# The first slot's rows in a routed feed-forward layer: gathered by a list of six columns instead of picked by products of one-hots

## The chip, the cores and the metric

The kernel runs on one core of one Trainium2 chip. The metric is device time in microseconds (us) for one execution. The kernel before takes 511.28 us, the median of three runs (511.26, 511.28 and 512.25).

## The reference

There are 2048 nodes with 256 values each and 67584 weighted edges. The kernel computes a graph layer and then a routed feed-forward layer on its result:

```
x = x + segment_sum(edge_weight[:, None] * layernorm(x)[dst], src) + node_vec1   # graph layer
t = layernorm(x)                                     # 2048 tokens of 256 values
logits = t @ Wr + br                                 # 8 experts
p, e = top_2(softmax(logits));  w = p / p.sum()
y_e = gelu((layernorm(t) * g_e + b_e) @ W1[e] + b1[e]) @ W2[e] + b2[e]      # 256 -> 1024 -> 256
x = x + w[0] * y_e[0] + w[1] * y_e[1]
```

(each token goes to two of eight experts, and each expert's weights are two matrices of 1 MB.)

## The kernel before

**Graph stage.** The edges are turned into dense 128-column blocks of an adjacency matrix, and the matrix product of these blocks with the normalised rows is summed into `acc`, which holds 16 blocks of 128 tokens. The blocks of the adjacency come in groups. `dense(blocks, b)` (line 368) issues the products of some groups for the two token blocks `b` and `b + 1` into a PSUM tile, and `add` (line 377) sums that tile into `acc`. The last of these products, for groups 4 and 3, run from line 1095 on and are interleaved with the routing, since token block after token block becomes final there.

**Routing.** The tokens are routed in two batches: the first has ten token blocks (`NA = 10`), the last has six. For a batch, in this order:

- `square` and `roots` (lines 692 and 703): ScalarE sums squares and takes roots.
- `scales` (711): reciprocals on VectorE; ScalarE writes the normalised rows into `rec`; SP stores the residual rows into `y_d` in memory.
- `logits`, `best` (twice), `shares` (724, 731, 773): the two best experts of each token and their odds. `shares` needs the Exp table on ScalarE.
- `count` and `sum_counts` (746, 760): which tokens chose which expert (`sel`), and, by products with a triangle of ones, how many earlier tokens chose the same expert. The result `pc` is a token's place in its expert's list.
- `set_shares` (779): the two weights go into the last columns of `rec`, and `rec` is stored in memory as `xr_d` by one DMA.
- `places` (788): the expert's list and the place in it, as two numbers per choice ("spots").
- `enlist` (803): one-hots of the two spot numbers, `in_lo` and `in_hi`, the latter times the token's number. `list_rows` (820): 20 products of these one-hots give `listed`, a table with the token number for every place in every expert's list.

**Slots.** The feed-forward layer runs over slots of 256 tokens of one expert. Three early slots (`whole[0]` to `whole[2]`, experts 0 to 2) are filled from the first batch alone, so that the layer can start before the second batch is routed. A slot needs its weights (`get_weights`, 939, on SP's queue), its rows (`get_rows`, 946: two indirect gathers of 128 rows each from `xr_d`, issued by GpSimd), `head` (974: four transposes of the rows on TensorE, `scale_rows` from PSUM into `xeT` on VectorE, `set_weights`), `layer_1` (1007: 16 products into eight PSUM tiles, each followed by a Gelu on ScalarE) and `layer_2` (1022: 16 products, `ys` on VectorE, an accumulating scatter into `y_d` by GpSimd).

**The first slot is filled in another way.** For `whole[0]` no rows are gathered for the products. `choose` (827) compares the places of expert 0 with 256 numbers and so makes one-hots `chosen`, ten blocks of 128 x 256; `choose_rows` (838) multiplies `rec` by them, 20 products, which gives the transposed rows at once:

```
for j in range(NA):
    for k in range(KD):
        nc.tensor.matmul(pt[:, k, :], s["rec"][:, j, k * P:(k + 1) * P], chosen[:, j, :], ...)
```

`early` (848) reads `listed` afterwards and gathers the rows of all three early slots, in the order 1, 0, 2. Those of slot 0 serve only its weights in `set_weights`.

**What sets the order.** From line 686 on the order on TensorE, VectorE, ScalarE and SP is the one in which the program issues the instructions (`manual_schedule`); GpSimd's queue holds here only the gathers and scatters. Every engine works its own queue in order, and waits at its head for semaphores of others. On TensorE the order around the change is: products of `dense` for token blocks 0 to 12, `sum_counts`, `dense` for blocks 14 and 15, `choose_rows`, `list_rows`, `layer_1` of slot 0, the transposes of slot 1, `layer_2` of slot 0 with the last batch's `sum_counts` in its middle.

Of the kernel before, what the change touches and what calls it, by code (L numbers as in the profile page):

```python
# [15 lines left out]
OP = mybir.AluOpType  # L16
# [11 lines left out]
def kernel(  # L28
# [339 lines left out]
    def dense(blocks, b):  # L368

        pa = ps_s.tile([P, 2, 512], F32, name="py1")  # L370
        for i in range(2):
            for c in blocks:
                nc.tensor.matmul(pa[:, i, :DX], acs[c][:, b + i, :], xn(c),  # L373
                                 start=(c == blocks[0]), stop=(c == blocks[-1]))
        return b, pa
# [310 lines left out]
    with tc.manual_schedule(engines=ALL - {ET.Pool}):  # L686
        listed = ps_r.tile([P, 2, P], F32, name="listed")
# [23 lines left out]
        def scales(s):  # L711
            b0 = s["b"]
            s["r"] = r = route.tile([P, 2, s["n"]], F32, name=f"r{s['i']}", bufs=1)
            nc.vector.reciprocal(r, s["sd"])  # L714
            ms = route.tile([P, s["n"]], F32, name=f"ms{s['i']}", bufs=1)
            nc.vector.tensor_mul(ms, less_m[:, b0:b0 + s["n"]], r[:, 1, :])
            s["rec"] = rec = route.tile([P, s["n"], RW], F32, name=f"rec{s['i']}", bufs=1)
            for j in range(s["n"]):
                nc.scalar.activation(rec[:, j, :D], acc[:, b0 + j, :D], AF.Identity,
                                     bias=ms[:, j:j + 1], scale=r[:, 1, j:j + 1])  # L720
            nc.sync.dma_start(y_d[:N, :].rearrange("(b p) d -> p b d", p=P)[:, b0:b0 + s["n"], :],
                              acc[:, b0:b0 + s["n"], :D])
# [23 lines left out]
        def count(s):  # L746

            hit = s["hit"]
            s["sel"] = sel = route.tile(s["full"], BF16, name=f"sel{s['i']}", bufs=1)
            nc.vector.tensor_add(sel, hit[:, :, 0, :], hit[:, :, 1, :])  # L750
            seen_b = route.tile([P, NE], BF16, name=f"seen_b{s['i']}", bufs=1)
            nc.vector.tensor_copy(seen_b, seen)
            s["seen"] = seen_b
            more = route.tile([P, NE], F32, name=f"more{s['i']}", bufs=1)
            nc.vector.tensor_reduce(more, sel.rearrange("p b e -> p e b"), AX.X, OP.add)
            nc.vector.tensor_add(seen, seen, more)
            s["seen_t"] = seen_t = route.tile([P, NE], BF16, name=f"seen_t{s['i']}", bufs=1)
            nc.vector.tensor_copy(seen_t, seen)

        def sum_counts(s):  # L760
# [10 lines left out]
            nc.tensor.matmul(s["all"], ones_b, s["seen_t"], start=True, stop=True)  # L771
# [7 lines left out]
        def set_shares(s):  # L779
            e, rec = s["odds"], s["rec"]  # L780
            both = route.tile([P, s["n"]], F32, name=f"both{s['i']}", bufs=1)
            nc.vector.tensor_scalar(both, e, 1.0, None, op0=OP.add)
            nc.vector.reciprocal(rec[:, :, D + 2], both)
            nc.vector.tensor_mul(rec[:, :, D + 3], e, rec[:, :, D + 2])
            nc.sync.dma_start(
                xr_d[:N, :].rearrange("(b p) c -> p b c", p=P)[:, s["b"]:s["b"] + s["n"], :], rec)
# [16 lines left out]
        def enlist(s):  # L803
# [3 lines left out]
            split = lambda t: t.rearrange("p n (a t) -> p n a t", t=2)  # L807
            each = iota_h[:, None, :].rearrange("p o (a t) -> p o a t", t=2).to_broadcast(hot)
            in_lo = route.tile([P, 2 * NA, P], F16, name="in_lo", bufs=1)[:, :n, :]
            nc.vector.tensor_tensor(split(in_lo), s["spots"][:, 0, :, None, :].to_broadcast(hot),  # L810
                                    each, OP.is_equal)
            in_hi = route.tile([P, 2 * NA, P], F16, name="in_hi", bufs=1)[:, :n, :]
            nc.vector.tensor_tensor(split(in_hi), s["spots"][:, 1, :, None, :].to_broadcast(hot),
                                    each, OP.is_equal)
# [3 lines left out]
            s["in"] = in_lo, in_hi  # L818
# [8 lines left out]
        def choose(s):  # L827

            pos = route.tile([P, NA], F32, name="pos", bufs=1)
            nc.vector.scalar_tensor_tensor(pos, s["pc"][:, :, 0], 1.0, s["sel"][:, :, 0],  # L830
                                           op0=OP.add, op1=OP.mult)
            for h in range(2):
                j = slice(h * NA // 2, (h + 1) * NA // 2)
                n = [P, NA // 2, TS]
                nc.vector.tensor_tensor(chosen[:, j, :], pos[:, j, None].to_broadcast(n),
                                        place1[:, None, :].to_broadcast(n), OP.is_equal)

        def choose_rows(s):

            pt = ps_x.tile([P, KD, TS], F32, name="px")  # L840
            for j in range(NA):
                for k in range(KD):
                    nc.tensor.matmul(pt[:, k, :], s["rec"][:, j, k * P:(k + 1) * P],  # L843
                                     chosen[:, j, :], start=(j == 0 and k == 0),
                                     stop=(j == NA - 1 and k == KD - 1))
            return pt

        def early(ps):
# [6 lines left out]
                tk, listed[:, 0, :].rearrange("p (e t) -> p e t", e=NE)[:, :EARLY, :TT],  # L855
# [5 lines left out]
            for u in (1, 0, 2):  # L861
# [3 lines left out]
            nc.scalar.copy(lists_0, listed[:, 0, :])  # L865

        def slots(ps):
# [39 lines left out]
            for i, r in spans:  # L907
# [25 lines left out]
        place1 = route.tile([P, TS], F32, name="place1", bufs=1)  # L933
        nc.gpsimd.iota(place1, pattern=[[1, TS]], base=1, channel_multiplier=0,
                       allow_small_or_imprecise_dtypes=True)
        chosen = route.tile([P, NA, TS], F32, name="chosen", bufs=1)
# [37 lines left out]
        def head(s):  # L974
# [8 lines left out]
            scale_rows(s, pt)  # L983
            set_weights(s)
# [92 lines left out]
        late.append(dense(GROUPS[4], 0))  # L1077
        for p in range(NP):
            if p + 1 < NP:
                late.append(dense(GROUPS[4] if 2 * p + 2 < NA else last, 2 * p + 2))  # L1080
# [3 lines left out]
            if p == NA // 2 - 1:  # L1084
                roots(first_b)
                scales(first_b)
                logits(first_b)
                best(first_b, 0)
            elif p == NA // 2:
                best(first_b, 1)  # L1090
                count(first_b)
                sum_counts(first_b)
                shares(first_b)
                nc.scalar.activation(warm, eps_sb, AF.Sqrt)
            elif p == NA // 2 + 1:
                choose(first_b)
# [3 lines left out]
        set_shares(first_b)  # L1100
        places(first_b)
        roots(last_b)
        enlist(first_b)
        pt = choose_rows(first_b)
        scale_rows(whole[0], pt)
        list_rows(first_b)
        hT = layer_1(whole[0])
        early(first_b["all"])
        scales(last_b)
        logits(last_b)  # L1110
# [4 lines left out]
        count(last_b)  # L1115
# [4 lines left out]
        enlist(last_b)  # L1120
        slots(last_b["all"])
        set_shares(last_b)
        hT = layer_1(whole[1], {4: lambda: list_rows(last_b)})
# [75 lines left out]
```

## Time and profile before

| | |
|---|---|
| median of three runs | 511.28 us |
| the profiled execution's own time | 512.25 us |
| its span, first to last instruction | 510.5 us |
| TensorE busy | 462.3 us (91% of the span) |
| VectorE, ScalarE, GpSimd busy | 278.2, 200.4, 154.7 us |
| mean granted TensorE clock | 0.982 of full |
| graph stage with routing of the first batch | up to about 248 us |
| slots | about 248 us to the end |

The profile is a record of one execution. Its times count from the first instruction of the span. An engine's busy share alone does not say what bounds a stage; the chain of waits does, which follows the work back from the last instruction. Matmul records carry the line of the source and the tiles' names; one fp32 product shows as two records, so that `choose_rows` with its 20 products is a row of 40. A row of the timeline has the start in us, the duration in us, the engine, the line, the operation, the tiles written and read, and in brackets how long the engine was idle before and what ended that. A wait for several semaphores is put down to one of them, which can be the wrong one. "SPq" is the DMA queue of SP: such a row is the issue of a DMA, not its data.

### The profile page before, as it was taken

Reading aid. Unit: us, or ns where it says so; the run is one execution under the profiler, and the core shown is the slowest. Engines: PE = TensorE matmul, PEld = TensorE weight load, DVE = VectorE, ACT = ScalarE, POOL = GpSimd, SP = SyncE. Lnnn points to the kernel's source line nnn. Section 1 sums busy time; section 2 is a strip of 40 time slices with the busy share of each in tenths; the row PEclk is TensorE's granted clock in tenths of the full one; section 3 lists DMA queues with packets and bytes.
Section 4 is the critical chain, followed back from the end, with each engine's and each line's share of the span. In section 5 each row is a group of like instructions: output and inputs, shape, how many; then the busy total and the mean of one; then the engine's idle time right before and its main releaser. Section 6 shows DMA issues by size and latency. Waiting matters only on the chain.

```text
span 510.5 us, 12148 instructions
## 1 busy us (share of the span) xinstructions
PE 462.3 (91%) x4996; PEld 394.0 (77%) x4996; DVE 278.2 (54%) x575; ACT 200.4 (39%) x489; POOL 154.7 (30%) x127
## 2 busy tenths in 40 slices
PE   1669989898999999899999999999999999996993
PEld 0557877676787887788878888888888888886882
DVE  5879899999999984347656122334332222121011
ACT  2355768662433221058272333332333333332220
POOL 5650506133040000000342433554334334422221
PEclk9999789999999999999999999999999999999898
DMA  3755577777656665991514996799998767739421
GB/s 111 221 166 163 189 219 239 219 215 242 212 172 190 202 183 172 346 322 67 163 41 104 342 339 173 233 347 365 349 342 263 208 157 205 217 90 319 139 88 35
DMA packets 87684, 106.82 MB, mean 209 GB/s; under 512 B 8656, under 2 KB 77376, under 8 KB 85504
## 3 DMA queue, kind: packets, MB, share of 16 engines
q1 hardware_dynamic: 79632, 92.08, 55.1%
q0 software_dynamic: 7952, 13.77, 11.3%
q8 instruction: 44, 0.72, 0.6%
q14 instruction: 24, 0.20, 0.1%
q10 hardware_dynamic: 32, 0.04, 0.0%
HBM read 79.85 MB, written 28.14 MB: 212 GB/s over the span
## 4 chain that ended last, share of the span: by engine, by line
PE 43%; DMA 10%; issue 2%; DVE 1%; SPq 0%; POOL 0%; POOLq 0%; ACT 0%; DVEq 0%
PE py L1030 18%; PE ph L1016 17%; DMA xs<-xr_d,to_i 7%; PE py L373 4%; PE px L843 2%; DMA out<-y_d 2%; PE px L981 1%; DMA y_rows<-out,to_i 1%; DMA out<-ys,to_i 0%; PE listed L824 0%; SPq L1168 0%; POOL out L1051 0%; POOLq L1195 0%; DVE in_hi L816 0%; DVE in_lo L810 0%
## 5 line engine op out<-in xcount | busy, mean ns | idle before, releaser
L1016 PE MATMUL ph<-xeT,w 128*128 128x256 f32 (+1 forms) x576 | 123.7, 371 | 5.6 <-PEq L1156 4.0
L1016 PEld LDWEIGHTS ph<-xeT,w 128*128 128x128 f32 x576 | 105.0, 192 | 20.3 <-issue 6.3
L1030 PE MATMUL py<-w,hT 128*128 128x256 f32 x544 | 120.6, 379 | 0.0
L1018 ACT ACTIVATE hT<-ph,ec 128x256 f32<-128x256 f32 (+1 forms) x144 | 65.9, 462 | 137.0 <-PE ph L1016 73.9
L1030 PEld LDWEIGHTS py<-w,hT 128*128 128x128 f32 x544 | 102.0, 190 | 13.2
L373 PE MATMUL py<-xn_lo,ac 128*128 128x264 f32 x352 | 85.1, 394 | 0.0
L1038 POOL DMA_INDIRECT y_d<-ys,to_i x30 | 48.9, 1631 | 114.7 <-DVE ys L1033 80.8
L320 DVE TENSOR_TENSOR hl<-k,iota_b 128x4096 bf16<-128x4096 bf16 x32 | 73.1, 2285 | 4.4 <-PE pa L359 2.2
L373 PEld LDWEIGHTS py<-xn_lo,ac 128*128 128x128 f32 x352 | 65.2, 191 | 12.5 <-ACT ar L362 0.2
L359 PE MATMUL pa<-hl,hr 128*32 128x128 bf16 x3072 | 61.3, 241 | 10.1 <-DVE hr L335 5.6
L359 PEld LDWEIGHTS <-hr 128*32 128x32 bf16 x3072 | 52.5, 108 | 21.7 <-issue 13.3
L1033 DVE SCALAR_TENSOR_TENSOR ys<-py,wt,b2w 128x256 f32<-128x256 f32 x34 | 16.4, 483 | 80.2 <-PE py L1030 65.6
L948 POOL DMA_INDIRECT xs<-xr_d,to_i x40 | 41.9, 1047 | 52.5 <-DVE r L714 32.8
L335 DVE TENSOR_TENSOR hr<-eq,w 128x3072 bf16<-128x3072 bf16 x32 | 56.3, 1758 | 2.5 <-ACT xT L399 0.5
L990 DVE TENSOR_SCALAR xeT<-px,ec 128x256 f32<-128x256 f32 (+1 forms) x38 | 18.4, 526 | 62.9 <-PE px L981 55.3
L362 ACT COPY ar<-pa 128x512 f32<-128x512 f32 x64 | 35.6, 585 | 31.7 <-PE pa L359 22.2
L240 POOL DMA_INDIRECT win_s<-in_src,at_i x8 | 11.3, 1418 | 87.9 <-DVE at_i L236 70.4
L378 DVE TENSOR_TENSOR acc<-acc,py 128x528 f32<-128x528 f32 x37 | 25.8, 700 | 22.2 <-PE py L373 22.2
L373 PE MATMUL py<-xn_hi,ac 128*128 128x264 f32 x160 | 36.2, 387 | 1.4 <-DVEq L588 1.4
L373 PEld LDWEIGHTS py<-xn_hi,ac 128*128 128x128 f32 x160 | 30.2, 190 | 6.8 <-issue 1.8
L1005 ACT ACTIVATE b2w<-b,wt 128x256 f32<-128x256 f32 x36 | 16.3, 500 | 27.9 <-DVE wt L1003 25.6
L327 DVE TENSOR_TENSOR eq<-k,iota_b 128x1024 bf16<-128x1024 bf16 x32 | 21.9, 683 | 0.0
(205 smaller groups left out, 336.3 us busy)
## 6 DMA issues: line engine op xcount, KB each, us to landing
w<-in_L_ffn_W SPq DMA_DIRECT2D x44, 1024.0 KB
ad<-ar SPq DMA_DIRECT2D x32, 512.0 KB
ac<-ad SPq DMA_DIRECT2D x16, 1024.0 KB
b<-in_L_ffn_b SPq DMA_DIRECT2D x22, 128.0 KB
acc<-in_x SPq DMA_DIRECT2D x4, 512.0 KB
out<-y_d SPq DMA_DIRECT2D x4, 512.0 KB
xr_d<-rec SPq DMA_DIRECT2D x1, 1300.0 KB
y_d<-acc SPq DMA_DIRECT2D x1, 1280.0 KB
```

Source lines behind the costliest of these rows:

```text
L320: nc.vector.tensor_tensor(hl.rearrange("p g (n t) -> p g n t", t=2), two(k2[:, 0], g, P), pair(P), OP.is_equal)
L327: nc.vector.tensor_tensor(eq.rearrange("p g (n t) -> p g n t", t=2), two(k2[:, 1], g, RK), pair(RK), OP.is_equal)
L335: nc.vector.tensor_tensor(hr.rearrange("p g i (n t) -> p (g i) n t", t=2), eq[:, :, None, :].to_broadcast([P, GH, 3, RK]), w[:, :, None, : ...
L359: nc.tensor.matmul(pa[j * RK:(j + 1) * RK, m, :], hr[:, g, i, :], hl[:, g, :], start=(i == 0), stop=(i == 2), tile_position=(0, j * RK))
L362: nc.scalar.copy(ar[:, m0:m0 + 4, :], pa)
L373: nc.tensor.matmul(pa[:, i, :DX], acs[c][:, b + i, :], xn(c), start=(c == blocks[0]), stop=(c == blocks[-1]))
L378: nc.vector.tensor_add(acc[:, b:b + 2, :], acc[:, b:b + 2, :], pa[:, :, :DX])
L948: nc.gpsimd.indirect_dma_start(out=(sets[s.set][0] if into is None else into)[:, t, :], out_offset=None, in_=(xr_d if rows is None else ro ...
L1016: nc.tensor.matmul(ph, w1[:, k, c * P:(c + 1) * P], xeT[:, k, :], start=(k == 0), stop=(k == KD - 1))
L1018: nc.scalar.activation(hT[:, c, :s.n * P], ph, AF.Gelu, bias=ec[:, c:c + 1], scale=1.0)
L1030: nc.tensor.matmul(py, hT[:, c, t * P:(t + 1) * P], w2[:, c, :], start=(c == 0), stop=(c == KH - 1))
L1038: st = nc.gpsimd.indirect_dma_start(out=y_d[:, :], out_offset=bass.IndirectOffsetOnAxis(ap=tos[s.to][:, t:t + 1], axis=0), in_=ys, in_offs ...
```

## The change

`choose` and `choose_rows` go. In their place a short list is made for the three early slots alone, and the rows of slot 0 are gathered and transposed like those of any other slot:

- `enlist` is split into `enlist_low` (`in_lo`, for the first batch in two instructions), `enlist_first` (one-hots of only six columns, two for each early slot, times the token number) and `enlist_high` (`in_hi`). `list_first` multiplies `in_lo` by the six columns, 20 small products, into a third part of `listed`. `early` reads that part.
- `dense` takes a table `between`: functions that are called ahead of a given product. The counts of the first batch now stand after three of the ten products for blocks 12 and 13 (before: after all ten), and the two halves of `list_first` after the first and the second of the ten for blocks 14 and 15.
- The Exp table is loaded ahead of the rows of `rec`, and `rec` is written in two parts, around the Exp itself. The store of `rec` is cut into three DMAs (blocks 0 to 3, 4 to 7, 8 and 9) and stands after `places` and `set_shares`.
- `seen_t` goes: the totals are summed on TensorE from `seen` and `sel`, with ten more small products in the first batch and six in the last.
- The full list (`enlist_high`, `list_rows`) is made later; its 20 products stand in `layer_1` of slot 0, ahead of its third PSUM tile.
- The early slots' rows are gathered in the order 0, 1, 2. Slot 0 gets `turn_rows`, that is the transposes and `scale_rows`, in place of `choose_rows`.
- The store of the last batch's residual rows keeps its place in `scales`, the writing of that batch's `rec` follows it as before.

The core of the diff, with lines left out:

```diff
+        def take_seen(s):
+            s["seen"] = seen_b = route.tile([P, NE], BF16, name=f"seen_b{s['i']}", bufs=1)
+            nc.vector.tensor_copy(seen_b, seen)
...
-            nc.tensor.matmul(s["all"], ones_b, s["seen_t"], start=True, stop=True)
+            nc.tensor.matmul(s["all"], ones_b, seen_b, start=True, stop=False)
+            for j in range(s["n"]):
+                nc.tensor.matmul(s["all"], ones_b, sel[:, j, :], start=False,
+                                 stop=(j == s["n"] - 1))
...
+        def put_recs(s, *cuts):
+            to = xr_d[:N, :].rearrange("(b p) c -> p b c", p=P)
+            for j, k in zip((0, *cuts), (*cuts, s["n"])):
+                nc.sync.dma_start(to[:, s["b"] + j:s["b"] + k, :], s["rec"][:, j:k, :])
...
+        def enlist_first(s):
+            n = s["n"] * 2
+            full = [P, n, EARLY * TT]
+            s["in_1"] = in_1 = route.tile(full, F16, name="in_1", bufs=1)
+            nc.vector.tensor_tensor(in_1, s["spots"][:, 1, :, 0:1].to_broadcast(full),
+                                    each_1[:, None, :].to_broadcast(full), OP.is_equal)
+            tk = tok1[:, s["b"]:s["b"] + s["n"], :].rearrange("p b (i t) -> p (b i) t", t=2)
+            nc.vector.tensor_tensor(in_1, in_1, tk[:, :, 0:1].to_broadcast(full), OP.mult)
+
+        def list_first(s, m0, m1):
+            for m in range(m0, m1):
+                nc.tensor.matmul(listed[:, 2, :EARLY * TT], s["in_lo"][:, m, :], s["in_1"][:, m, :],
+                                 start=(m == 0), stop=(m == 2 * s["n"] - 1))
...
-            for u in (1, 0, 2):
+            for u in range(EARLY):
...
-        late.append(dense(GROUPS[4], 0))
-        for p in range(NP):
...
-            elif p == NA // 2 + 1:
-                choose(first_b)
+        roots(first_b)
+        nc.scalar.activation(warm, eps_sb, AF.Exp)
+        scales(first_b)
+        scale_recs(first_b, range(0, 5))
+        logits(first_b)
+        best(first_b, 0)
+        best(first_b, 1)
+        shares(first_b)
+        scale_recs(first_b, range(5, NA))
+        select(first_b)
+        late.append(dense(last, NA + 2, {(0, last[3]): lambda: sum_counts(first_b)}))
+        sum_up(NL)
+        places(first_b)
+        set_shares(first_b)
+        put_recs(first_b, 4, 8)
+        enlist_first(first_b)
+        enlist_low(first_b, NA)
+        nc.scalar.activation(warm, eps_sb, AF.Sqrt)
+        late.append(dense(last, NA + 4, {(0, last[1]): lambda: list_first(first_b, 0, NA),
+                                         (0, last[2]): lambda: list_first(first_b, NA, 2 * NA)}))
+        early(first_b["all"])
+        sum_up(NL + 1)
+        enlist_high(first_b)
+        count(first_b)
+        take_seen(last_b)
+        sum_up(NL + 2)
...
-        set_shares(first_b)
-        places(first_b)
         roots(last_b)
-        enlist(first_b)
-        pt = choose_rows(first_b)
-        scale_rows(whole[0], pt)
-        list_rows(first_b)
-        hT = layer_1(whole[0])
-        early(first_b["all"])
+        turn_rows(whole[0])
+
+        def list_batch_0():
+            list_rows(first_b)
+            nc.scalar.copy(lists_0, listed[:, 0, :])
+
+        hT = layer_1(whole[0], {2: list_batch_0})
```

(`sum_up(p)` is `add` of the oldest PSUM tile followed by the two `square`s; `NL` is 5; `last` is the five blocks of groups 3 and 4.)

## The prediction

> **What bounds the kernel now.** First the chain of waits in order of time, around the change:
>
> ```profile
> 215.91 18.04 PE py L373 x80
> ...
> 234.26 4.56 PE py L373 x20
> 238.82 8.63 PE px L843 x40
> 247.45 1.12 PE listed L824 x20
> 248.57 6.96 PE ph L1016 x32
> ```
>
> TensorE runs here without a gap: from 215.91 to 255.53 each piece starts where the one before ends, and the slots behind continue so. In the list of waits TensorE idles after 216 only 1.3 us (for `in_hi`), twice 0.4 us, and 0.7 and 4.0 us at branches near the end. So what leaves this stretch of TensorE's queue brings everything behind it forward by as much, and each wait put into it costs in full. Rates from these rows: one record of `dense` takes 18.04/80 = 0.2255 us, one of L843 8.63/40 = 0.216, one small product of the list 1.12/20 = 0.056.
>
> **What leaves, and what must be ready instead.** The 8.63 us of L843 go. `choose`'s VectorE work (2.89 us from 234.85) goes too, but TensorE did not wait for it. The first layer may then start once the last `dense` ends, if slot 0's rows are there. Before, the rows came straight from `rec`; now they go to memory and back. I follow that path, with durations from the timelines of VectorE, SP and GpSimd:
>
> ```profile
> 231.98 0.24 DVE L750 TENSOR_TENSOR sel<-hit 128x80 bf16<-128x80 f32 x1
> ...
> 240.02 0.31 DVE L791 TENSOR_TENSOR at_e<-hit,counts 128x160 f32<-128x160 f32 x1
> ...
> 241.46 1.49 DVE L810 TENSOR_TENSOR in_lo<-spots,iota_h 128x2560 f16<-128x2560 f16 x1
> ```
> ```profile
> 240.18 0.37 SPq L785 DMA_DIRECT2D xr_d<-rec  x1
> ```
> ```profile
> 253.43 1.00 POOL L948 DMA_INDIRECT xs<-xr_d,to_i  x1 [0.30 <-issue]
> ```
> ```profile
> 256.35 0.23 DVE L1000 TENSOR_SCALAR mine<-xs,iota_p 128x4 f32<-128x4 f32 x1 [2.71 <-DMA xs<-xr_d,to_i]
> ```
>
> 1. `sel`. The first `best` and all before it keep their times. The `add` of 0.62 us that stood between the two `best` moves behind `sel`, the subtraction of `shares` comes ahead: `sel` ends about 231.8 instead of 232.22.
> 2. Counts. TensorE has done three of the ten products for blocks 12 and 13 by 229.44 + 6 x 0.2255 = 230.8 and waits until 231.9. Behind that wait stand the other seven products. Twelve count products took 0.32 us (233.94 to 234.26), so 22 take 0.59. The last `dense` ends at 231.9 + 0.6 + 14 x 0.2255 + 20 x 0.2255 + 20 x 0.056 = **241.25**, against 238.82: the list's 20 products (0.5 us by the counts' row, 1.1 by L824; their weights are as wide as L824's, so 1.1) and the wait are in it.
> 3. Places and weights. `add`, then `places`, from at_e to `in_lo` 1.44 us, then `set_shares` 0.63: from 232.5 to 234.6. ScalarE has Exp's table ready at 229.0 (1.28 us load behind the roots that end 227.5), five rows at 0.5, the Exp at 231.8, five rows by 234.4: just in time.
> 4. Store of `rec`. Issue 234.7. Before, it was issued at 240.18, and the record by fifths of a us has its first bytes at 241.05; 1.33 MB at the 350 GB/s moved there are 3.8 us. Cut in three, it moves no faster: all three wait for `set_shares`, and the gathers for all three. Last byte 239.35. For the completion I take 0.45 us, by the stores of `ad`, whose follower is issued 0.4 to 0.5 us after their last byte (189.3 to 189.82); some of them had a thin tail of up to 1.4 us, which is the upper end; the lower is 0.4. Landed: **239.8** (to 241.2).
> 5. The list. `in_1` (two of about 0.3 us) and `in_lo` (two halves of 0.83) end 236.8, the list's products 237.65, the row numbers about 238.4. That is 1.4 us ahead of the store: the list isn't what is late.
> 6. Gathers. 253.43 to 256.35 says: 1.00 us of GpSimd, then 1.92 us until a reader starts; two follow at 1.30. From 239.9, unhindered: second landed 239.9 + 1.3 + 1.0 + 1.9 = 244.1.
>
> Here a row speaks against the plan: VectorE makes `in_hi` now, two instructions of 1.49 us, from 239.25 to 242.16. Early in the kernel the same kind of gather stood beside such two-input operations of VectorE:
>
> ```profile
> 76.43 0.94 POOL L240 DMA_INDIRECT win_s<-in_src,at_i  x1 [14.86 <-DVE at_i L236]
> 77.68 2.17 POOL L240 DMA_INDIRECT win_d<-in_dst,at_i  x1 [0.30 <-issue]
> ```
> ```profile
> 76.74 2.29 DVE L320 TENSOR_TENSOR hl<-k,iota_b 128x4096 bf16<-128x4096 bf16 x1
> ```
>
> The second gather ends 0.82 us after the operation in whose course it began (79.03 to 79.85). The Trainium skill ("SBUF — State Buffer", SBUF: two separate sides) says that GpSimd is shut out of a shared port until VectorE's operation ends and is free about 0.115 us later. By that figure the second gather would end at 242.3, by the row (0.82, plus 0.06 as these gathers take 1.00 instead of 0.94) the first ends 240.74 + 0.88 = 241.6 and the second 242.16 + 0.88 = 243.05. I take the row: landed 243.05 + 1.92 = 245.0.
> 7. Transposes and evictions. The second pair 0.27, `xeT` 0.5 until TensorE may start, 0.1 of handing over: the first layer starts at **245.9**. L824's 1.12 us used to hide this eviction; now nothing does. VectorE's own queue (`in_hi`, counts, the last `add`) is empty at 243.5, so it isn't late. Behind the wait for the transposes stands the last batch's routing, which ScalarE's roots release at 245.2 anyway.
>
> **Sum with an even clock.** Start 248.57 before, 245.9 after: 2.67 won. Given back: `list_rows` inside the layer, 1.12, and six more count products in `layer_2`, 6 x 0.027 = 0.16. Net **1.4 us won**. What follows (ScalarE's rows of `rec`, its table loads, the scaled biases, for which the first `ys` waits at 262.6) is tied to the first layer and moves with it; the copy of the list even leaves that stretch.
>
> **The clock.** TensorE now idles from 241.25 to 245.9, 4.65 us, but for two transposes of 0.2. The trace has one such gap, near the end:
>
> ```profile
> 472.31 8.64 PE L1016 MATMUL ph<-xeT,w 128*128 128x256 f32 x32 [4.02 <-PEq L1156]
> ```
> ```profile
> 470.00:471.00 1.00, 0.00 (x0) 0.00 (x0) 0.00 (x0) 0.00 (x0) 0.00 (x0) 1.00 1.15 274
> ...
> 473.00:474.00 1.00, 1.00 (x4) 0.82 (x3) 0.00 (x0) 0.00 (x0) 0.90 (x1) 0.50 0.00 0
> ```
>
> In the second fence the number after the bracket of the last engine is the granted clock: 1.00 while TensorE idles, 0.50 when it starts again; it is full again at about 475.3. The layer took 8.64 us where the same row elsewhere takes 7.07 with its tail: **1.6 us lost**. Gaps of 1.40 us (at 214.5) and 1.26 us (at 267) cost nothing. The Trainium skill ("TensorE: Matmul & The Clock Gate", Part 1) has a free-running window of about 3.4 us: an idle one halves the clock, a busy one restores it; and by its Part 4 transposes hardly count as busy. Taken literally, an idle stretch of 4.65 holds a whole window in (4.65 - 3.41)/3.41 = 36% of runs; by the row, 4.02 us were enough, and the clock also halved at 52.2 and 65.9 in windows that were only part idle. I lean to the row and take 75%. Cost between 1.1 (half the slow window falls into the idle) and 2.3 (two slow windows); I take 1.6. By the rule alone the sum would be won by about 0.8 on the mean; by the row it is 1.4 - 1.6 = -0.2, **0.2 us lost**.
>
> Against the profiled execution's own 512.25 (span 510.5) that is 512.45; against the median of the runs, 511.28, which lies 0.97 lower, **511.5**.
>
> **The rivals.**
>
> - *The clock holds* (transposes or a lucky window). For it: the rule's 36%; against: the 4.02 us gap. 1.4 won, by the bounds of steps 4 and 6 0.6 to 2.2: **509.9**.
> - *The gathers miss their turn beside VectorE.* One mechanism: if the store lands later than 240.7, the end of `in_hi`'s first operation, the first gather begins in the second operation, is held to 243.05, and the second, free, ends 244.35: landed 246.3, start 247.2, and the 786 KB of the last residual store (issued 243.5, data from about 244.4) get in its way. Then an even clock leaves 0.1 won, and 6 us idle cost 1.6 to 2.3: about 1.9 lost, **513.2**. For it: the tail on some stores; against: the store of `rec` before ended without one (53 GB/s in the us from 247).
> - *The change does not free TensorE at all:* VectorE's queue is the bound. It would be empty at 243.5 and start the layer at 244.5, so it cannot be late unless gathers are earlier than I have them; then 1.5 us more are won, **508.5** at an even clock. Small.
>
> **Chances and range.** A measurement of this kernel can tell about 0.2%, 1.0 us, from no change. My forecast (0.2 lost, from 510.5 to 512.6 by its own bounds) has 0.45, the steady clock 0.22, the late gathers 0.28, VectorE's bound 0.05. The forecast's edge beyond 512.3 goes to slower, and the weaker end of the steady clock to the same: faster 0.23, same 0.44, slower 0.33. The range takes in the steady clock and most of the late gathers: 509.5 to 513.4.
>
> **What would show it.** In the changed profile: no L843; a gap on TensorE ahead of the transposes of slot 0, from about 241.3, in which the list of waits names the gather or `xeT`; gathers from 239.9, each near 1.7 and 1.2 us instead of 1.0; the first layer's row at 245.9, with 0.50 in the granted clock and 8 to 9 us instead of 6.96 for the matmuls besides the list; `list_rows` in its middle. Wrong would I be if the row numbers, not the store, released the first gather, if the gap were under 3 us, or if the granted clock stayed at 1.00 behind 4 us or more of idle.

## The result, and the profile after

The kernel became slower: 515.26 us at the median of seven runs (513.70 to 516.89) against 511.26 of seven runs before on the same chip (509.77 to 512.25), a ratio of 1.0086 with a 95% interval of 1.0063 to 1.0109. 511.5 was predicted, with 509.5 to 513.4 as the range. The profiled execution took 515.51 us with a span of 513.7. Across experiments ratios are compared, not times, since every kernel took some 6 us more while e8 to e10 ran, and the ratios leave out runs in a slow state of the chip: four of e10's 14, its profiled one among them, five of the 35 of the kernel before beside it, and two of e12's 22.

The whole span is a poor ruler here. TensorE comes back to the `dense` products behind the graph's loop at 215.91 us before and at 212.87 after, although the change touches nothing ahead of that, and in the other profiles at 212.5 to 223.2. So I measure a **count**: from this return to the first product of the second slot's layer 1. Before, 263.00 - 215.91 = 47.09 us. After, 264.83 - 212.87 = 51.96. The change costs **4.87 us** there, where the prediction had 0.2. What follows moves with that point: from there to the first layer of a slot 191 us later TensorE takes 190.99 to 191.14 us in 11 of the 14 profiles.

TensorE's rows of the kernel before that this rests on:

```profile
248.40 7.13 PE L1016 MATMUL ph<-xeT,w 128*128 128x256 f32 x32
...
263.00 3.62 PE L1016 MATMUL ph<-xeT,w 128*128 128x256 f32 x16
```

TensorE's timeline of the changed kernel (start, duration, engine, line, operation; the bracket is the idle time ahead and what ended it):

```profile
212.87 14.93 PE L375 MATMUL py<-xn_hi,ac 128*128 128x264 f32 x66 [1.39 <-DVEq L590]
228.76 0.21 PE L772 MATMUL counts<-sel,before 128*128 128x80 bf16 x1 [0.97 <-ACT e L788]
...
234.04 3.81 PE L375 MATMUL py<-xn_hi,ac 128*128 128x264 f32 x16
242.04 0.69 PE L995 MATMUL px<-ident,xs 128*128 128x128 f32 x2 [4.19 <-DMA xs<-xr_d,to_i]
244.97 0.69 PE L995 MATMUL px<-ident,xs 128*128 128x128 f32 x2 [2.24 <-DMA xs<-xr_d,to_i]
246.30 3.78 PE L1033 MATMUL ph<-xeT,w 128*128 128x256 f32 x8 [0.64 <-DVE xeT L1007]
249.87 2.10 PE L861 MATMUL listed<-in_hi,in_lo 128*128 128x128 f16 x20
251.81 5.40 PE L1033 MATMUL ph<-xeT,w 128*128 128x256 f32 x24
...
264.83 3.62 PE L1033 MATMUL ph<-xeT,w 128*128 128x256 f32 x16
```

L843 is gone, and in its place stands a gap. The last `dense` ends at 237.85, layer 1 starts at 246.30. The rows of slot 0 come in two parts: TensorE waits 4.19 us for the first gather and 2.24 for the second. Counted from the return, layer 1 starts at 33.43 us; before it was 248.40 - 215.91 = 32.49, and 29.99 was predicted. (The prediction took 248.57 for the row before, from the chain of waits, which counts a row from the end of the one ahead; all starts here are the timeline's.) Then layer 1 with the list takes 10.91 us (246.30 to 257.21).

The queues of SP and GpSimd in the same stretch:

```profile
231.57 2.03 SPq L800 DMA_DIRECT2D xr_d<-rec  x3
239.71 0.36 SPq L721 DMA_DIRECT2D y_d<-acc  x1
```
```profile
238.84 1.02 POOL L962 DMA_INDIRECT xs<-xr_d,to_i  x1 [41.18 <-DVE more L765]
240.16 1.00 POOL L962 DMA_INDIRECT xs<-xr_d,to_i  x1 [0.30 <-issue]
```

The store of the records is issued at 231.57 and the first gather starts 7.27 us later. The bracket names VectorE as its releaser, which e1 below shows to be wrong. The gathers take 1.0 us each, unstretched. The last residual store (L721, 786 KB) is issued between them.

And windows of one us (busy time of PE, PEld, DVE, ACT, POOL; then the granted clock, the DMA engines' share, GB/s):

```profile
241.00:242.00 1.00, 0.00 (x0) 0.00 (x0) 0.00 (x0) 0.98 (x3) 0.69 (x2) 0.67 0.80 290
242.00:243.00 1.00, 0.69 (x2) 0.29 (x2) 0.00 (x0) 0.69 (x1) 0.69 (x2) 0.50 1.10 391
...
250.00:251.00 1.00, 1.00 (x12) 1.00 (x11) 0.74 (x6) 0.47 (x1) 0.00 (x0) 0.50 0.00 0
251.00:252.00 1.00, 1.00 (x13) 1.00 (x11) 0.00 (x0) 0.00 (x0) 0.00 (x0) 0.71 0.00 0
```

The clock is halved from about 241.3 to about 251.6, some 10 us. The DMA engines are full in 242 to 243, when slot 0's rows should come.

### The profile page after: what moved, and what is told of

The parts are those of the page before. It is cut to its first block, busy times and chain, and to the rows that moved or that the text cites. A ratio compares the mean times of both kernels' runs of the same rounds, so it can differ in the third digit from the quotient of the medians.

```text
span 513.7 us, 12149 instructions
## 1 busy us (share of the span) xinstructions
PE 455.1 (89%) x4996; PEld 387.7 (75%) x4996; DVE 274.4 (53%) x571; ACT 200.6 (39%) x490; POOL 156.3 (30%) x127
## 4 chain that ended last, share of the span: by engine, by line
PE 39%; DMA 11%; DVE 3%; issue 2%; ACT 1%; POOL 0%; SPq 0%; POOLq 0%; DVEq 0%; ACTq 0%
PE py L1047 18%; PE ph L1033 17%; DMA xs<-xr_d,to_i 8%; PE py L375 3%; DMA out<-y_d 2%; PE px L995 2%; DMA y_rows<-out,to_i 1%; PE listed L861 1%; DVE in_hi L853 0%; DMA out<-ys,to_i 0%; DVE in_hi L850 0%; SPq L1204 0%; ACT b2w L1022 0%; DVE xeT L1007 0%; DVE acc L380 0%
## 5 line engine op out<-in xcount | busy, mean ns | idle before, releaser
L1033 PE MATMUL ph<-xeT,w 128*128 128x256 f32 (+1 forms) x576 | 127.2, 379 | 6.3 <-PEq L1192 4.1
L1033 PEld LDWEIGHTS ph<-xeT,w 128*128 128x128 f32 x576 | 107.2, 196 | 22.0 <-issue 5.5
L320 DVE TENSOR_TENSOR hl<-k,iota_b 128x4096 bf16<-128x4096 bf16 x32 | 73.1, 2284 | 2.5 <-PE pa L359 2.5
L359 PE MATMUL pa<-hl,hr 128*32 128x128 bf16 x3072 | 56.1, 235 | 8.7 <-DVE hr L335 6.7
L359 PEld LDWEIGHTS <-hr 128*32 128x32 bf16 x3072 | 49.3, 105 | 18.4 <-DVE hr L335 9.0
L362 ACT COPY ar<-pa 128x512 f32<-128x512 f32 x64 | 35.3, 585 | 26.4 <-PE pa L359 20.3
```

Source lines behind the costliest of these rows:

```text
L320: nc.vector.tensor_tensor(hl.rearrange("p g (n t) -> p g n t", t=2), two(k2[:, 0], g, P), pair(P), OP.is_equal)
L359: nc.tensor.matmul(pa[j * RK:(j + 1) * RK, m, :], hr[:, g, i, :], hl[:, g, :], start=(i == 0), stop=(i == 2), tile_position=(0, j * RK))
L362: nc.scalar.copy(ar[:, m0:m0 + 4, :], pa)
L1033: nc.tensor.matmul(ph, w1[:, k, c * P:(c + 1) * P], xeT[:, k, :], start=(k == 0), stop=(k == KD - 1))
```

## The experiments

All are cut from the changed kernel. Here are the counts, with the medians and, in brackets, the kernel before timed beside it:

| run | median us (before) | ratio, 95% interval | count us | layer 1 starts at |
|---|---|---|---|---|
| before | | | 47.09 | 32.49 |
| the change | 515.26 (511.26) | 1.0086, 1.0063 to 1.0109 | 51.96 | 33.43 |
| e1 in_hi later | 513.99 (510.30) | 1.0071, 1.0051 to 1.0091 | 51.24 | 32.29 |
| e2 store later | 512.66 (510.30) | 1.0055, 1.0032 to 1.0078 | 48.47 | 30.93 |
| e3 idle products | 516.56 (510.30) | 1.0108, 1.0074 to 1.0141 | 50.60 | 34.69 |
| e4 list in the gap | 513.59 (510.30) | 1.0073, 1.0044 to 1.0102 | 50.02 | 33.07 |
| e5 = e2 + e4 | 511.91 (510.68) | 1.0036, 1.0020 to 1.0052 | 47.29 | 30.95 |
| e6 = e5 + idle products | 510.96 (510.68) | 1.0015, 0.9997 to 1.0033 | 47.00 | 32.19 |
| e7 = e6 + early rows | 512.48 (510.68) | 1.0029, 1.0011 to 1.0047 | 47.04 | 32.22 |
| e8 = e6, copy later | 522.07 (517.04) | 1.0114, 1.0071 to 1.0157 | 52.35 | 35.01 |
| e9 = e8 + early rows | 519.03 (517.04) | 1.0039, 1.0016 to 1.0062 | 49.64 | 33.16 |
| e10 = e5 + early rows | 516.19 (517.04) | 0.9959, 0.9924 to 0.9994 | 48.41 | 30.95 |
| e11 = e10, in_hi first | 510.58 (510.07) | 1.0012, 0.9997 to 1.0027 | 47.67 | 30.55 |
| e12 = e10 again | 509.63 (510.07) | 0.9980, 0.9962 to 0.9997 | 47.23 | 30.77 |

The medians are of all runs. The two last columns are of one profiled execution each and count from TensorE's return. e10 and e12 are the same kernel, and their counts lie 1.18 us apart, so a smaller difference between two counts shows nothing by itself. Counts and ratios don't tell quite the same: in e2, e3, e5 and e7 the ratio stands for 1.4 to 2.0 us more than the count has. Where the other runs spend this isn't shown.

**e1: does VectorE hold the first gather?**

```diff
         sum_up(NL + 1)
-        enlist_high(first_b)
...
         turn_rows(whole[0])
+        enlist_high(first_b)
...
-        hT = layer_1(whole[0], {2: list_batch_0})
+        hT = layer_1(whole[0], {6: list_batch_0})
```

> VectorE's two long in_hi operations (1.48 and 1.49 us, ended 0.38 us before the first gather of the changed kernel) are moved behind xeT, and list_rows from the third to the seventh chunk of layer 1. Theory that VectorE holds the gathers back: the first gather starts 1.5 to 2.2 us earlier, counted from the last dense product's end (it was 0.63 us behind that end, 7.27 us behind the first issue of the records' store), layer 1 starts 1 to 2 us earlier, the kernel takes about 1.5 us less, 513.8. Rival, the store's landing releases the first gather: it stays 7.3 us behind the store's issue, and the time stays within 0.5 us of 515.3.

Timelines of e1, SP and GpSimd, then TensorE:

```profile
232.18 2.02 SPq L800 DMA_DIRECT2D xr_d<-rec  x3
```
```profile
240.20 1.02 POOL L962 DMA_INDIRECT xs<-xr_d,to_i  x1 [41.92 <-ACT sq L696]
```
```profile
244.01 1.12 PE L995 MATMUL px<-ident,xs 128*128 128x128 f32 x4 [5.56 <-DMA xs<-xr_d,to_i]
```

With VectorE out of the way, the first gather does not come earlier, it comes later: 8.02 us behind the issue instead of 7.27. So the store's landing releases it, as the rival says. The trace's records of packets and semaphores show what the landing is made of, counted from the issue:

| run | last packet ends | GpSimd passes its first wait for the store | first gather |
|---|---|---|---|
| the change | 5.29 | 6.34 | 7.27 |
| e1 | 6.56 | 7.09 | 8.02 |
| e2 | 5.28 | 5.83 | 6.75 |
| e3 | 6.51 | 7.12 | 8.04 |
| e4 | 6.57 | 7.10 | 8.03 |
| e5 | 5.28 | 6.10 | 7.03 |

In e1, e3 and e4 the last four to six packets come up to 1.3 us after the others. The packet records show what stands there: one packet of 16 KB, of a queue of the kind "instruction" (q8), takes 0.96 us, and the late packets follow within 0.02 us of its end, so they very likely shared its DMA engine. It begins 5.00 to 5.10 us behind the issue in these three, and 5.28 to 5.29 in the change, e2 and e5, where the store's packets are through. Then 0.5 to 1.1 us pass until the wait ends, and always 0.92 to 0.94 us from there to the gather: three waits in a row and a MOVE. The time expected by the first theory, 513.8, was nearly met (513.99), but not by its mechanism; the ratio, 1.0071, doesn't differ from the change's beyond their intervals. In e1 the residual store's bytes had passed before the rows came, so that all four transposes ran together, 1.49 us behind the second gather's end.

**e2: the last residual store.** It is issued by ScalarE's queue inside layer 1:

```diff
             s["ms"] = ms
-            nc.sync.dma_start(y_d[:N, :].rearrange("(b p) d -> p b d", p=P)[:, b0:b0 + s["n"], :],
-                              acc[:, b0:b0 + s["n"], :D])
+            if b0 == 0:
+                put_sums(s, nc.sync)
...
+        def put_sums(s, queue):
+            b0 = s["b"]
+            queue.dma_start(y_d[:N, :].rearrange("(b p) d -> p b d", p=P)[:, b0:b0 + s["n"], :],
+                            acc[:, b0:b0 + s["n"], :D])
...
             nc.scalar.copy(lists_0, listed[:, 0, :])
+            put_sums(last_b, nc.scalar)
```

> Only the store of the last residual sums (786 KB) moves, from 239.7 us to ScalarE's queue behind list_rows, inside layer 1 of slot 0. Theory that this store gets in the rows' way: the rows of the second gather land about 1.9 us behind its end instead of 3.8, layer 1 starts 1.5 to 2 us earlier, the time falls by 1.5 to 2 us to about 513.5. Rival, the four gathers of slots 1 and 2 crowd each other: the second pair of transposes still starts 3.5 us or more behind the second gather's end, and the time stays within 0.5 us of 515.3.

TensorE and GpSimd in e2:

```profile
241.08 0.69 PE L1000 MATMUL px<-ident,xs 128*128 128x128 f32 x2 [3.37 <-DMA xs<-xr_d,to_i]
242.34 0.69 PE L1000 MATMUL px<-ident,xs 128*128 128x128 f32 x2 [0.57 <-DMA xs<-xr_d,to_i]
243.66 3.57 PE L1038 MATMUL ph<-xeT,w 128*128 128x256 f32 x8 [0.64 <-DVE xeT L1012]
```
```profile
239.52 1.00 POOL L967 DMA_INDIRECT xs<-xr_d,to_i  x1 [0.30 <-issue]
```

The second gather ends at 240.52 and its transposes start at 242.34: 1.82 us instead of 3.81. The gathers of slots 1 and 2 still follow, so it was the store and not they. The packets agree: in e1, e3 and e4, where the store's packets stand ahead, the first gather's rows begin to move 2.40 to 3.47 us behind its start, in e2 and e5 1.72. Layer 1 starts 2.50 us earlier on the count: 1.99 from this, 0.51 from a gather that started earlier, as the landing differs from run to run. One us more is won behind it, since the clock comes back at 246.9, after two windows of some 3.4 us and not three. These 3.49 us are the largest step of the count. In the time the step is smaller, 1.0086 to 1.0055 or 1.6 us, and the two intervals overlap.

**e3: idle products.** 122 products of 128x128 that nobody reads fill the gap, added work only:

```diff
+        def fill(n):
+            for _ in range(n):
+                nc.tensor.matmul(listed[:, 0, :], ones_b, iota_b, start=True, stop=True)
...
-        turn_rows(whole[0])
+        fill(70)
+        turn_rows(whole[0], 36)      # 36 between the two tiles' transposes
+        fill(16)
```

> 122 bf16 products of 128x128 without use (70 behind the last dense product, 36 between the two tiles' transposes, 16 ahead of layer 1) fill TensorE's gap; nothing else changes. Theory that the gap halves the clock: it stays near 1.00, layer 1 of slot 0 with list_rows takes about 8.1 us instead of 10.9 and the transposes half of 0.69 each pair; the time falls by 2.5 to 3 us to about 512.5. Rival, the low clock there is a matter of the run's phases and not of the gap: layer 1 again takes 10 us or more and the time does not fall.

```profile
247.51 0.44 PE L999 MATMUL px<-ident,xs 128*128 128x128 f32 x2 [2.40 <-DMA xs<-xr_d,to_i]
...
250.92 1.95 PE L1039 MATMUL ph<-xeT,w 128*128 128x256 f32 x8
252.70 1.28 PE L861 MATMUL listed<-in_hi,in_lo 128*128 128x128 f16 x20
253.81 5.40 PE L1039 MATMUL ph<-xeT,w 128*128 128x256 f32 x24
```

The granted clock is 1.00 in every half us of the stretch. Layer 1 with the list takes 8.29 us (250.92 to 259.21) instead of 10.91. So the halved clock costs **2.62 us**, and the gap is its cause. The time did not fall at all (ratio 1.0108), and there the rival was right. In the profile late packets put the gather 0.76 us back, the second transposes came only straight behind the filler, and TensorE's return was 3.4 us later than in the change's; why the median of the four runs stayed up, one profile cannot say. Only the count shows the gain.

**e4: the list in the gap.**

```diff
-        turn_rows(whole[0])
-        hT = layer_1(whole[0], {2: list_batch_0})
+        list_rows(first_b)
+        nc.scalar.copy(lists_0, listed[:, 0, :])
+        turn_rows(whole[0])
+        hT = layer_1(whole[0])
```

> list_rows stands ahead of the transposes, in the gap that TensorE has anyway, instead of inside layer 1. Theory: layer 1 becomes 1.9 us shorter (what list_rows took there at the low clock), the rest stays, the time falls by 1.1 to 1.9 us to about 513.7; if the products in the gap also end the clock's low windows earlier, by another 1 us. Rival: list_rows waits for in_hi in front of the transposes and the rows come no earlier, so that layer 1 starts later by 1 us and the time stays within 0.7 us of 515.3.

```profile
238.17 1.28 PE L861 MATMUL listed<-in_hi,in_lo 128*128 128x128 f16 x20 [0.67 <-DVE in_hi L853]
243.57 1.39 PE L995 MATMUL px<-ident,xs 128*128 128x128 f32 x4 [4.13 <-DMA xs<-xr_d,to_i]
245.60 9.33 PE L1033 MATMUL ph<-xeT,w 128*128 128x256 f32 x32 [0.64 <-DVE xeT L1007]
```

The list ran at 238.17, in a gap that lasted until 243.57 anyway. Layer 1 took 9.33 us instead of 10.91 with the list, and the count fell by 1.94. So the theory holds on the count. Part of it is the clock: two windows were halved here, not three. The ratio fell by 0.13% only, within the intervals.

**e5 and e6: do the parts add, and what remains?** e5 joins the edits of e2 and e4. e6 adds 61 idle products around the list and between the transposes.

> The last residual store moves into layer 1 (ScalarE's queue) and list_rows into the gap. Counted from TensorE's return to the dense products behind the graph's loop to the first product of the second slot's layer 1: 47.09 us before the change, 51.96 with it, 48.47 with the store alone moved and 50.02 with list_rows alone moved. Theory that the two losses add: 48.47 less the 1.1 us of list_rows, 47.3, and a time within 1 us of the kernel before (ratio about 1.001), with the granted clock still 0.50 over most of layer 1. Rival, they overlap in one loss: 48.4 again, ratio about 1.005.

> As the run with store and list_rows moved, with 61 bf16 products of 128x128 without use around list_rows and between the transposes, sized so that they end before the rows come. Theory that what remains is the halved clock: it stays near 1.00, transposes and layer 1 take some 1.8 us less, 45.5 us on that count, about 1.5 us faster than the kernel before (ratio about 0.997). Rival, the fillers hold up the transposes or the clock falls all the same: 47 us or more, ratio 1.000 or more.

First e5, then e6:

```profile
243.62 8.72 PE L1038 MATMUL ph<-xeT,w 128*128 128x256 f32 x32 [0.64 <-DVE xeT L1012]
```
```profile
241.79 1.61 PE L995 MATMUL listed<-iota_b,ones_b 128*128 128x128 bf16 x26 [1.79 <-ACT lists L1148]
...
245.28 7.19 PE L1044 MATMUL ph<-xeT,w 128*128 128x256 f32 x32
```

e5: 47.29, as added up beforehand (47.3). But the time missed: a ratio of 1.0036 instead of 1.001, nearer to the rival's 1.005. And the clock is halved for one window only, from about 243.4 to 246.8, not over most of layer 1. e6: at the full clock layer 1 takes 7.19 us, 1.53 less than in e5, but it starts 1.24 later, because the idle products had to wait for ScalarE's copy of the list out of the same tile and then stood in front of the transposes. So e6 shows again what the clock costs, and as a version it gains nothing: 47.00 and 1.0015, as the rival had it.

**e7: fewer bytes behind the shares.** The first five blocks' rows go out when ScalarE has scaled them:

```diff
         scale_recs(first_b, range(0, 5))
+        put_x(first_b, 0, 5)                 # 256 of 260 columns
...
-        put_recs(first_b, 4, 8)
+        put_rest(first_b, 5)                 # 4 columns of blocks 0-4, then blocks 5-9 whole
```

> As the run before it, and the first five blocks' record rows (256 of 260 columns) are stored as soon as ScalarE has scaled them, ahead of the shares; behind the shares follow their four last columns (640 packets of 16 bytes) and the other five blocks' whole rows. Theory that the bytes of the store behind the shares set the first gather (6.8 to 8.0 us from issue to gather for 1.33 MB): with 0.67 MB the gather starts 1 to 1.9 us earlier, the count falls to 44.5 or less (ratio about 0.995). Rival, small packets cost as much as they save or the fixed part of the round trip dominates: gather 6.5 us or more behind the issue, 45.5 us or more.

SP and GpSimd in e7:

```profile
233.61 0.36 SPq L808 DMA_DIRECT2D xr_d<-rec  x1
```
```profile
239.06 1.02 POOL L976 DMA_INDIRECT xs<-xr_d,to_i  x1 [39.30 <-DVE in_hi L864]
```

The first gather starts 24.10 us behind the return (25.71 in e5, 26.83 in e6) and 5.45 behind the first issue that follows the shares. The theory of the bytes holds for the gather. The count stays at 47.04 and the ratio at 1.0029, both missed, for the same idle products in the way as in e6.

**e8 and e9: the copy moved behind the idle products.** e8 is e6 with ScalarE's copy behind the transposes and 59 idle products; e9 is e8 with the early rows and 37 of them.

> As the run with 61 idle products, which had waited 1.79 us for ScalarE's copy of the list and so held up the transposes; here the copy stands behind them, and 59 products remain. On the same count (TensorE's return to the dense products to the second slot's layer 1; 47.09 before the change, 47.00 in that run): layer 1 starts 1.2 us earlier, 45.1 to 46.2 us, ratio 0.997 to 1.000. Rival, the rows come that late anyway: 47.0 again.

> As the run before it with the first five blocks' record rows stored ahead of the shares, and 37 idle products. Theory that the store's bytes behind the shares decide: the first gather 24.1 us behind TensorE's return (25.7 to 26.8 with the whole store), layer 1 at about 29.3, the count about 44.2, 2.9 us less than before the change, ratio about 0.994. Rival, layer 1 then waits for something else (xeT behind the last add, the gathers' landing): 45.5 or more.

Both missed, by 6 and 5 us. The list of waits of e8 (total us, times, longest):

```profile
DVE xeT L1018 <- remote: 7.6, 1, 7.6
ACT lists L1151 <- remote: 6.0, 1, 6.0
...
PE ph L1044 <- DVE xeT L1018: 3.1, 1, 3.1
```

VectorE and ScalarE wait here for TensorE alone ("remote": nothing in the profile released them). In e9 the last transposes end at 249.65, but TensorE's semaphore is recorded at 253.44. Why it came 3.8 us late isn't settled. The same kind of wait stands in the profile before, in the graph's stage (2.1 and 1.9 us, at L320 and L362), also behind long rows of short bf16 products. These two runs say nothing about the row path.

**e10 to e12: only real work.** e10 is e5 with e7's early rows, and e12 is the same kernel again. e11 makes `in_hi` ahead of the row numbers, so that VectorE is not at it while GpSimd gathers.

> The run before it without the idle products: only real work on TensorE. The gap is then about 3 us wide on either side of list_rows. Theory of the clock: it halves in one or two windows, layer 1 takes 1 to 2 us longer, count 45.2 to 46.2, ratio 0.997 to 0.999. Rival, the gap is now too short for the clock to fall: 44.2, as with the idle products.

> As the run with the early record rows and no idle products (its first gather took 2.15 us instead of 1.0 under VectorE's second in_hi operation; count 48.41, with layer 1 at the halved clock for 9.84 us), but VectorE makes in_hi before it makes the row numbers, so that no long operation of VectorE lies beside the gathers and list_rows needs not wait for it. Theory that VectorE stretches the gathers: all six take 1.0 us, the first ends 25.3 to 26.1 us behind TensorE's return to the dense products (26.5 in that run), layer 1 starts at 29.7 to 30.4 (30.95), count 44.5 to 47 depending on the clock, ratio about 0.996. Rival, the row numbers become late instead: the first gather starts more than 25.5 us behind that return, and the count is 48 or more.

> The same kernel as the run with the early record rows and no idle products, timed a second time beside the other order of in_hi, because the runs there lay up to 12 us apart. If its ratio of 0.996 holds, it lies between 0.993 and 0.999 again; if that was chance, at 1.000 to 1.003, which its count of 48.4 against 47.1 would give.

GpSimd and VectorE in e12:

```profile
237.42 1.95 POOL L976 DMA_INDIRECT xs<-xr_d,to_i  x1 [39.74 <-DVE in_hi L864]
```
```profile
236.98 1.49 DVE L867 TENSOR_TENSOR in_hi<-in_hi,tok 128x2560 f16<-128x2560 f16 x1
```

The early gather now falls into VectorE's second `in_hi` and lasts 1.95 us instead of 1.0 (2.15 in e10). It ends 0.90 us after that operation's end. e11 takes that away: all gathers take 1.0 us, but the row numbers are ready only at 237.48, the first gather starts at 25.06, and layer 1 starts 0.22 earlier than in e12. The gathers went as expected; the count, 47.67, did not fall below 47, and the ratio, 1.0012, missed the 0.996. The clock still halves in all three, for one window in e12 and two in e10 and e11 (layer 1 takes 8.84, 9.84 and 9.50 us). So the clock hides what the gathers gain, and e10 missed its count (48.41 instead of 45.2 to 46.2).

Twice the interval of the early-rows version lies below 1 (0.9924 to 0.9994, 0.9962 to 0.9997). It is the only one for which that holds, by some 0.2 to 0.4%; the medians of all runs give 0.1 to 0.2%. Its count, 47.23, does not show where: it is 0.14 above that of before. I take it for about level, and where the rest comes from stays open.

## Why the prediction was wrong, step by step

What failed first is the landing of the store (step 4); behind it failed the landing of the rows (step 6) and the price of the clock.

- **Steps 1 to 3, 5: right.** Seen from TensorE's return, `sel`, the wait of 0.97 us before the counts and `set_shares` came within 0.1 us of their times. The last `dense` ended 0.4 earlier (24.98 behind the return): ten of the list's products, six columns wide, moved `dense` on by 0.26 us, not 0.55. The row numbers were ready at 234.85, well ahead of the store.
- **Step 4, the landing: the term that failed first.** Issue and rate were right (231.57, and the bulk of the packets done 4.9 us later). I counted 0.45 us for the completion and nothing for GpSimd's own start. Measured were a last packet at 5.29 instead of 4.65, 0.5 to 1.1 of completion and 0.93 of start: 7.27 us from issue to gather instead of 5.2. The upper end that I had named (1.4 us of tail) was the better value. The stores of `ad` were the wrong row, since SP's next issue stood behind them, not GpSimd's waits. Effect: the first gather 1.98 us later than predicted.
- **Step 6, VectorE's hold: wrong here, right in kind.** With the store that late, both `in_hi` operations were over, the second 0.38 us before, and the gathers ran free, 0.83 us better than forecast. e10 and e12 show the hold where the gather does fall in: it ends 0.9 us behind the operation, as the row had it (0.82, and 0.06 for the longer gather). The 0.115 us of the Trainium skill ("SBUF — State Buffer", "A bandwidth-pool intuition that's wrong") is how long behind VectorE's end GpSimd stays blocked. I had taken it for the end of the gather, which may have work left by then, so these runs don't contradict it.
- **Step 6, the rows' landing: 3.81 us instead of 1.92.** The residual store was named in the rival, not in the forecast. Seen from the return it was issued 0.75 us earlier than predicted and the gather came 1.98 later, so the two met. e2 shows that the store is the cause; that an earlier gather would have escaped it wasn't run. 1.89 us.
- **Step 7: 0.43 more,** as a pair of transposes takes 0.69 at the halved clock (0.44 in e3) and I had 0.27. With the three terms above, 1.98 - 0.83 + 1.89 + 0.43 = 3.47; measured is layer 1 at 33.43 instead of 29.99, 3.44 us.
- **The clock: right in kind, too small.** I took 1.6 us with bounds of 1.1 and 2.3, for a gap of 4.65 us. The gap became 8.4 us, and three windows were halved instead of one or two: 2.62 us by e3. I had fixed the price of the clock from one gap of 4.02 us. The last section shows that the same gap can cost one window or two. The working had a slip besides: its 36% is the share in which the clock falls by the rule, so the rule gave the steady clock 64%, and the rival that names 36% in its favour had it the wrong way round.
- **`list_rows`: the size held.** 1.12 us were booked as given back. At the full clock layer 1 to the second slot's start is 15.91 us (e3) against 263.00 - 248.40 = 14.60 before: 1.31, of which 0.19 are left for the counts (0.16 booked). e4 shows on the count that its place was the loss, as the gap next to it was empty.

The 4.87 us divide into 0.94 (layer 1 later than before) + 2.62 (clock) + 1.31 (list and counts). That sum closes by construction, as the three are cut from the same rows. Against the prediction's 0.2 the difference is 3.44 for the later start, 1.02 for the clock, 0.03 for list and counts and 0.17 for the reading of the row before.

The rival of the late gathers (513.2, with 0.28 of the chance) had the late landing and the residual store right and the hold beside VectorE wrong, and was still too cheap by 2 us. The range failed because I added its parts as if they were independent. A later store lengthens the gap, can put the rows behind the residual store, and can give the clock another window: one delay, paid up to three times. e1 sets a limit to this reading: its gather came later still, yet the second rows came 1.49 us behind their gather.

## What to carry to other kernels

A round trip through memory has a price behind its bytes (here 1.5 to 2 us from the last packet to the gather), and it is read at the engine that waits, not at another queue's next issue. Before moving a transfer onto the critical path, look at which large transfer is issued just then for no hurry; moving this one away won 3.5 us on the count, more than any other edit, though the time shows only 1.6 of it. If an idle gap of TensorE cannot be avoided, put the work there that stands behind it, and price the halved clock in windows, with one more than the gap seems to need as the upper end.

## What the hardware showed that was not expected

- The clock changes in these traces only in steps of 3.41 us. Here are such windows of the change, then of e5 (first number behind the comma: us in which TensorE was busy; 1.00 or 0.50 ahead of the last two: the granted clock):

```profile
237.93:241.34 3.41, 0.00 (x0) 0.00 (x0) 1.68 (x5) 1.53 (x6) 2.02 (x2) 1.00 0.18 31
241.34:244.76 3.42, 0.69 (x2) 0.29 (x2) 0.00 (x0) 1.33 (x2) 2.68 (x3) 0.50 0.99 322
244.76:248.17 3.41, 2.56 (x7) 1.80 (x8) 2.26 (x10) 0.00 (x0) 1.30 (x2) 0.50 0.42 111
248.17:251.58 3.41, 3.41 (x22) 2.87 (x20) 2.33 (x13) 0.95 (x2) 0.00 (x0) 0.50 0.00 0
```
```profile
239.97:243.38 3.41, 0.87 (x4) 0.40 (x4) 0.36 (x1) 2.60 (x8) 2.72 (x3) 1.00 0.42 117
243.38:246.79 3.41, 3.17 (x8) 2.52 (x9) 3.03 (x15) 0.47 (x1) 2.00 (x2) 0.50 0.36 95
246.79:250.21 3.42, 3.42 (x17) 3.03 (x16) 1.20 (x8) 1.84 (x4) 0.00 (x0) 1.00 0.40 143
```

  A window at the full clock need not be wholly idle to be followed by a halved one: in e5 a quarter busy was little enough. In the change a halved window that was busy for 75% was followed by another halved one, in e5 one of 93% by the full clock. Around the gap ahead of layer 1 and the one near the end, in all 14 profiles, 21 windows that were busy for 0 to 44% were followed by a halved one and one of 41% was not; none of 46% or more was. A halved stretch went on behind every window busy for 81% or less and ended behind every one of 82% or more.
- So the length of a gap alone does not give its price. The gap near the end lasts 3.72 to 4.48 us in 11 profiles and halved the clock each time, for one window in eight of them and for two in three:

```profile
474.36 10.06 PE L1033 MATMUL ph<-xeT,w 128*128 128x256 f32 x32 [4.10 <-PEq L1192]
```

  That is the change; the kernel before has 4.02 us of gap and 8.64 for the same row, and at the full clock it takes 7.14 (e6). So these 1.42 us of the changed kernel's profile are most likely chance and not the change. Ahead of layer 1 three windows were halved in the change and e1, two in e2, e4, e10 and e11, one in e5 and e12, none in e3, e6 and e7 with their idle bf16 products; in e8 and e9 the late semaphore left a gap behind these, and two and one were halved. The Trainium skill ("TensorE: Matmul & The Clock Gate", Part 4) says that transposes don't count as activity in the way other products do; the 0.69 us of each pair are too short to test that here.
- The last packets of a store were 1.3 us late in three of the six runs of the table, behind one 16 KB packet of the instruction queue.
- 640 packets of 16 bytes went out in 0.45 us (e7), far cheaper than the 0.67 MB they stood for; as many bytes of the other five blocks took 2.1 us.
- TensorE's semaphore came 3.8 us late behind idle products in e9; the reason is open.
